# The last 32 columns of a two-layer image kernel kept in SBUF by mask slot, and stored by an indirect DMA in the middle of the output loop

## The chip, the cores and the metric

The kernel runs on one core of a Trainium2 chip. The metric is the device time of one execution in microseconds; the time given for the kernel is the median of several executions. One execution was also taken with the hardware profiler; "the trace" is its record, and all single durations come from it.

## The reference

The input x is one image of 512 x 512 positions with 64 channels, float32. Two layers follow, both residual:

```
# layer 0: x = x + L0(gn(x))
xn    = ln(gn(x))                                  # group norm over the image, layer norm over channels
left  = (xn @ left_w  + left_b)  * mask * sigmoid(xn @ lgate_w + lgate_b)
right = (xn @ right_w + right_b) * mask * sigmoid(xn @ rgate_w + rgate_b)
out   = ln(einsum('bkjd,bkid->bijd', left, right)) @ out_w + out_b
L0    = out * sigmoid(xn @ ogate_w + ogate_b)
# layer 1: x = x + L1(gn(x)); L1 keeps 12 x 12 Fourier modes
x_ft  = fft2(gn(x))[:12, :12];  out_ft = einsum('bcmn,comn->bomn', x_ft, w)
L1    = real(ifft2(out_ft, padded to 512 x 512))
```

`mask[i, j] = m[i] * m[j]` for a sequence mask m of 512 zeros and ones. Group norm has 32 groups of two channels; its statistics run over the whole image, so layer 1 cannot begin its correction before the last tile of layer 0 is done.

## The kernel before, in words

**Slots and ranks.** The kernel sorts the 512 image rows by the mask: a row's *rank* is its place in that order, and a *slot* is a place in it. Layer 0 works on slots, four blocks of 128 (b = 0 to 3) on the 128 partitions. `src_i[:, b, jc]` holds, for each slot, the index of its row's chunk jc of 32 columns in x (row index times 16, plus jc). A tile is one block of 128 rows times 32 columns times 64 channels; in SBUF it has 8 KB on each partition, 1,048,576 bytes in all. There are 16 column chunks (NJ) x 4 blocks = 64 tiles.

**Layer 0's last stage** (the loop over s, lines 1137 to 1251; its order is written out by hand, step by step, and each engine's queue holds the instructions in that order) runs over 32 units, a unit being one column chunk and two blocks: `units[k] = (jc, half)`. A unit is loaded by two gathers (POOL's queue, line 1038) into one of five places of the big SBUF tensor `places` (`x_of(k)`, line 976, ring of RING = 5), is transposed, gated and added up there (POOL's `added`, line 1056; the last unit's end on VectorE, `finished`, line 1060), and stays until three things have read it: TensorE's `transform` (line 1079, the forward row transform with the basis `hb`, which is in slot order), VectorE's `statistics` (line 1109), and the `store` (line 1071), which writes its two tiles to DRAM on SP's queue. The DRAM copy is `x1_h`, two tensors of 256 columns each (line 54), with rows in slot order. Units 0 to 29 are stored at their own step, unit 31 at line 1230 after everything else.

**Layer 1's end** (lines 1253 to 1393). `group_norm_affine` (line 1297) ends the statistics; `mixed_ps` (line 1311) multiplies the modes; `back_columns(jb)` (line 1329) makes the inverse transform along the columns for four chunks (jb = 0 to 3, into `parts`): jb = 0 before the loop, the others inside it. Then the output loop goes over the 64 tiles in the order of the rows of the image: chunk jc outer, block b inner, where b now counts *image rows*, not slots. So each tile has to be fetched from `x1_h` by rank: `fetch_rows` (line 939) is an indirect gather on POOL's queue with `dst_i` (line 832), rank times 8 plus the chunk's place in its tensor. For each tile TensorE multiplies the row basis `rinv` (in row order) with `parts` into four PSUM tiles `l_ps` (line 1377), VectorE adds each to the tile (line 1384), and SP stores the tile directly (line 1385).

```
ahead = 4 * jc + b + AHEAD
if ahead < len(tiles_left):
    fetch_rows(ahead)
```

**What sets the order around the change.** The fetched tiles live in a ring of AHEAD = 15 buffers (`buffers`, lines 933, 1261 to 1265): parts of `places` that are free by then, five tiles `lx_t`, and two spare pieces. Three gathers are issued during the last units (line 1187), twelve after the loop over s (line 1266); in that part the places 0 and 1, which hold units 30 and 31, serve as four buffers once they are stored. In the output loop the gather for position i + 15 is issued after tile i, into tile i's buffer, so POOL waits for that store to land. POOL's queue is in order, and so is SP's. The DMAs of POOL's queue (q0, made by software) use eight semaphores in turn, and so do SP's (q1).

Of the kernel before, what the change touches and what calls it, by code (L numbers as in the profile page):

```python
# [10 lines left out]
I32 = mybir.dt.int32  # L11
# [18 lines left out]
JC = 32  # L30
NJ = N // JC
K = 2 * P
AHEAD = 15
# [13 lines left out]
def conv_preact_kernel(ctx: ExitStack, tc: tile.TileContext, t: dict):  # L47
# [5 lines left out]
    x1_d = dram.tile([N, N, C], F32, name="x1_d")  # L53
    x1_h = [dram.tile([N, HALF, C], F32, name=f"x1_h{h}") for h in range(2)]
    fwd_d = dram.tile([M2, N, C], F32, name="fwd_d")
# [14 lines left out]
    src_i = const.tile([P, 4, NJ], I32, name="src_i")  # L70
    few_i = const.tile([P, NJ // 2], F32, name="few_i")
    n_i = const.tile([1, 1], I32, name="n_i")
    with tc.tile_pool(name="ix", bufs=1) as xp, tc.tile_pool(
# [17 lines left out]
        pick = load_const("c_pick", [P, G])  # L91
        nc.sync.dma_start(few_i, t["c_iota"][:, : NJ // 2])
        nc.vector.tensor_copy(table[:, :, 1], mask_i32)
# [527 lines left out]
    def compact(fc):  # L621
# [201 lines left out]
        with tc.tile_pool(name="tri", bufs=1) as trp:  # L823
# [3 lines left out]

            dst_i = fc.tile([P, 4, NJ // 2], I32, name="dst_i")
            base = fc.tile([P, 4], F32, name="dst_base")
            nc.vector.tensor_scalar(base, rank_p, float(NJ // 2), None, ALU.mult)  # L830
            for b in range(4):
# [49 lines left out]
            with tc.manual_schedule(), tc.tile_pool(name="late", bufs=1) as lp:  # L881
# [50 lines left out]
                free = 3 * 64 * C + C * MODES * MODES  # L932
                buffers = [place(7)[:, JC:], places[:, free : free + JC * C].rearrange("p (n c) -> p n c", c=C)]
                buffers += [place(2)[:, r * JC : (r + 1) * JC] for r in range(2)]
                ranked = [h.rearrange("s (k j) c -> (s k) (j c)", k=NJ // 2) for h in x1_h]
                tiles_left = [(jc, b) for jc in range(NJ) for b in range(4)]
                fetched = {}

                def fetch_rows(i):
                    jc, b = tiles_left[i]  # L940
                    fetched[jc, b] = buffers[i % AHEAD]
                    gather(fetched[jc, b].rearrange("p j c -> p (j c)"), ranked[jc // 8], dst_i, b, jc % 8)

# [3 lines left out]
                with tc.tile_pool(name="np_x", bufs=LEAD + 2) as tp, tc.tile_pool(  # L947
# [123 lines left out]
                    def store(k, r):  # L1071
                        jc, half = units[k]
                        b = 2 * half + r
                        nc.sync.dma_start(
                            x1_h[jc // 8][b * P : (b + 1) * P, (jc % 8) * JC : (jc % 8 + 1) * JC, :].rearrange("p j c -> p (j c)"),
                            x_of(k)[:, r * JC : (r + 1) * JC].rearrange("p j c -> p (j c)"),
                        )
# [59 lines left out]
                    for s in range(-LEAD, total_g + 2 * SIZE):  # L1137
# [3 lines left out]
                        def held(i):  # L1141
                            return 0 <= v - i < len(units)
# [44 lines left out]
                        if (v, n) in ((last - 2, 3), (last - 1, 3), (last, 3)):  # L1187
                            fetch_rows(len(fetched))
                        if v == last and 2 <= n < 6:
# [63 lines left out]
                with tc.tile_pool(name="lq", bufs=1) as qp, tc.tile_pool(name="lx0", bufs=1) as xp0, tc.tile_pool(  # L1253
# [6 lines left out]
                    for i, xp in enumerate(xps):  # L1260
                        buffers += [xp.tile([P, JC, C], F32, name=f"lx_t{i}_{j}") for j in range((2, 2, 1)[i])]
                        if i > 0:
                            buffers += [place(i - 1)[:, r * JC : (r + 1) * JC] for r in range(2)]
                    spare = places[:, 7 * 64 * C - 8 * 2 * MODES * M2 : 7 * 64 * C]
                    buffers += [spare[:, i * JC * C : (i + 1) * JC * C].rearrange("p (n c) -> p n c", c=C) for i in range(2)]
                    for i in range(len(fetched), AHEAD):
                        if i == 8:
                            nc.gpsimd.memset(picks, 0.0)
                        fetch_rows(i)
                    pick4 = qp.tile([P, 4], F32, name="pick4")  # L1270
                    nc.scalar.dma_start(pick4, t["c_pick4"])
# [4 lines left out]
                    with tc.tile_pool(name="sps", bufs=1, space=PSUM) as sps:  # L1276
# [12 lines left out]
                        def join_modes(ab):  # L1289
                            nc.vector.tensor_add(v[:, 0], sums[:, :, :MODES], turned[:, :, MODES:])  # L1290
                            nc.vector.tensor_sub(v[:, 1], turned[:, :, :MODES], sums[:, :, MODES:])
                            for k in range(2):
                                h = slice(k * C, (k + 1) * C)
                                one = v[h, k, 0, 0:1]
                                nc.vector.scalar_tensor_tensor(one, ab[h, 2:3], float(N * N), one, ALU.mult, ALU.add)

                        ab2 = group_norm_affine(lp, sets, 8, "x1c", turn_sums, join_modes)
# [68 lines left out]
                    with tc.tile_pool(name="lpq", bufs=2, space=PSUM) as pq, tc.tile_pool(  # L1366
                        name="lpt", bufs=2, space=PSUM
                    ) as pt, tc.tile_pool(name="lps", bufs=4, space=PSUM) as pp:
                        for jc in range(NJ):
                            for b in range(4):  # L1370
                                it = parts[:, jc // 8, (jc % 8) * N : (jc % 8 + 1) * N]
                                xt = fetched.pop((jc, b))
                                group = []
                                for g in range(4):
                                    ps = pp.tile([P, JC, 16], F32, name="l_ps")
                                    h = slice(32 * g, 32 * g + M2)
                                    nc.tensor.matmul(  # L1377
                                        ps.rearrange("p j o -> p (j o)"), rinv[h, b, :], it[h],
                                        start=True, stop=True, tile_position=(32 * g, 0),
                                    )  # L1380
                                    group.append(ps)
                                for g, ps in enumerate(group):
                                    os_ = slice(16 * g, 16 * g + 16)
                                    nc.vector.tensor_add(xt[:, :, os_], xt[:, :, os_], ps)  # L1384
                                nc.sync.dma_start(  # L1385
                                    out[0, b * P : (b + 1) * P, jc * JC : (jc + 1) * JC, :].rearrange("i j c -> i (j c)"),
                                    xt.rearrange("p j c -> p (j c)"),
                                )
# [82 lines left out]
```

## Time and profile before

| what | value |
|---|---|
| median of 3 runs | 1818.94 us (1818.11 to 1819.47) |
| the profiled execution | 1816.82 us |
| its span, first to last instruction | 1815.0 us |
| TensorE busy | 1641.3 us (90%) |
| VectorE busy | 1424.5 us (78%) |
| ScalarE busy | 961.3 us (53%) |
| POOL busy | 945.1 us (52%) |
| DMA, whole run | 467.94 MB, mean 258 GB/s |
| last VectorE statistics of layer 0 end | 1498.6 us |
| first store of the output loop issued (SP) | 1528.22 us |
| last VectorE add of the output loop ends | 1787.25 us |

The busy shares are means over stages that differ. The page's slices cut the span in 40 pieces of 45.4 us; their digits are busy tenths. The chain of waits follows the work that ended last backwards, from each instruction to what released it. In a timeline line the columns are start, duration (both us), engine, line, operation, output and inputs, count, and in brackets the idle time before it and what ended it. The table by stage gives, for a stretch of time, its length, the busy time and number of instructions of TensorE's matmuls, its weight loads, VectorE, ScalarE and POOL, then TensorE's granted clock, the share of the 16 DMA engines in use, and GB/s.

### The profile page before, as it was taken

Reading aid. Unit: us, or ns where it says so; the run is one execution under the profiler, and the core shown is the slowest. Engines: PE = TensorE matmul, PEld = TensorE weight load, DVE = VectorE, ACT = ScalarE, POOL = GpSimd, SP = SyncE. Lnnn points to the kernel's source line nnn. Section 1 sums busy time; section 2 is a strip of 40 time slices with the busy share of each in tenths; the row PEclk is TensorE's granted clock in tenths of the full one; section 3 lists DMA queues with packets and bytes.
Section 4 is the critical chain, followed back from the end, with each engine's and each line's share of the span. In section 5 each row is a group of like instructions: output and inputs, shape, how many; then the busy total and the mean of one; then the engine's idle time right before and its main releaser. Section 6 shows DMA issues by size and latency. Waiting matters only on the chain. (4 is left out here: it accounts for less than half of the span.)

```text
span 1815.0 us, 33640 instructions
## 1 busy us (share of the span) xinstructions
PE 1641.3 (90%) x11424; PEld 1287.8 (71%) x11424; DVE 1424.5 (78%) x2980; ACT 961.3 (53%) x1708; POOL 945.1 (52%) x711
## 2 busy tenths in 40 slices
PE   6779899999899999998999999999999977998772
PEld 6667666664688778897888888888888844665331
DVE  7989777777455547779999999999999996765442
ACT  3666555554222259986777777777777741011000
POOL 4665111111000006788999999999999892211120
PEclk9989999999899999999999999999999986555555
DMA  7999155556655513577777776777677689999999
GB/s 286 386 386 380 72 138 137 140 140 153 203 176 184 175 47 133 213 256 254 259 239 242 265 246 234 256 267 260 238 259 271 220 261 418 425 427 426 427 426 385
DMA packets 189525, 467.94 MB, mean 258 GB/s; under 512 B 34848, under 2 KB 134176, under 8 KB 148384
## 3 DMA queue, kind: packets, MB, share of 16 engines
q1 hardware_dynamic: 158160, 262.09, 42.5%
q0 software_dynamic: 27712, 201.40, 29.0%
q10 hardware_dynamic: 3472, 2.20, 0.5%
q8 instruction: 93, 1.52, 0.3%
q14 instruction: 88, 0.72, 0.1%
HBM read 278.05 MB, written 187.56 MB: 257 GB/s over the span
## 5 line engine op out<-in xcount | busy, mean ns | idle before, releaser
L995 PE MATMUL w_ps<-gate_x,xt_c 128*128 128x128 f32 x2048 | 281.1, 281 | 28.9 <-DVE z_t L1211 27.3
L1058 POOL TENSOR_TENSOR places<-places,z_t 128x1024 f32<-128x1024 f32 x127 | 301.0, 2370 | 8.1
L995 PEld LDWEIGHTS w_ps<-gate_x,xt_c 128*128 128x128 f32 x2048 | 252.6, 194 | 45.1 <-DVE z_t L1211 43.6
L995 PE MATMUL c_ps<-center_x,xt_c 128*128 128x128 f32 x2048 | 277.6, 279 | 1.2 <-ACT xt_c L1024 0.6
L995 PEld LDWEIGHTS c_ps<-center_x,xt_c 128*128 128x128 f32 x2048 | 253.6, 195 | 3.9 <-ACT xt_c L990 2.8
L1377 PE MATMUL l_ps<-places,rinv 24*128 24x512 f32 x512 | 207.4, 1127 | 30.1 <-DVE places L1384 18.8
L1113 DVE BATCH_NORM_STATS2 stats2c<-places 128x6 f32<-128x128 f32 x1024 | 220.4, 278 | 8.4 <-POOL places L1058 8.4
L1028 DVE TENSOR_REDUCE scratch<-sq_c 128x16 f32<-128x1024 f32 x160 | 194.5, 1216 | 27.9 <-ACT sq_c L1023 19.4
L1215 POOL TENSOR_TENSOR z_t<-z_t,bias_row_out 128x1024 f32<-128x1024 f32 x32 | 75.6, 2364 | 247.8 <-DVE z_t L1211 243.7
L1162 ACT ACTIVATE z_t<-z_t 128x1024 f32<-128x1024 f32 x128 | 135.5, 1058 | 130.6 <-DVE z_t L1217 129.1
L985 PE MATMUL t_ps<-c_ident,places 128*128 128x128 f32 x1280 | 199.6, 279 | 1.3 <-DVE places L870 1.3
L1377 PEld LDWEIGHTS l_ps<-places,rinv 24*128 24x128 f32 x512 | 120.3, 304 | 112.3 <-DVE places L1384 57.0
L985 PEld LDWEIGHTS t_ps<-c_ident,places 128*128 128x128 f32 x1280 | 145.1, 142 | 60.6 <-issue 52.9
L990 ACT ACTIVATE xt_c<-t_ps,ab_xc 128x512 f32<-128x512 f32 x256 | 176.0, 687 | 13.2 <-PE t_ps L985 12.1
L1211 DVE TENSOR_TENSOR z_t<-w_ps,rs_n 128x512 f32<-128x512 f32 x256 | 171.9, 672 | 8.3 <-PE w_ps L995 8.2
L1020 ACT ACTIVATE sq_c<-c_ps 128x512 f32<-128x512 f32 x256 | 150.5, 588 | 32.5 <-PE c_ps L995 32.0
L1217 DVE TENSOR_TENSOR z_t<-z_t,scratch 128x1024 f32<-128x1024 f32 x128 | 156.3, 1221 | 9.9 <-ACT rs_n L1034 3.7
L687 DVE BATCH_NORM_STATS2 stats1c<-x_ps 128x6 f32<-128x512 f32 x256 | 156.6, 682 | 8.0 <-PE x_ps L686 7.6
L1054 POOL TENSOR_TENSOR z_t<-z_t,places 128x1024 f32<-128x1024 f32 x64 | 151.5, 2368 | 13.9 <-ACT z_t L1162 13.8
L1384 DVE TENSOR_TENSOR places<-places,l_ps 128x512 f32<-128x512 f32 x176 | 109.2, 682 | 55.8 <-DMA places<-x_h,dst_i 43.9
L1054 POOL TENSOR_TENSOR z_t<-z_t,bias_row_out 128x1024 f32<-128x1024 f32 x63 | 149.3, 2370 | 5.7 <-ACT z_t L1162 5.4
L749 POOL COPY rbc<-rq_out 128x512 f32<-128x512 f32 x64 | 38.3, 613 | 210.2 <-DVE rq_out L214 132.0
(213 smaller groups left out, 2746.9 us busy)
## 6 DMA issues: line engine op xcount, KB each, us to landing
x_h<-places SPq DMA_DIRECT2D x64, 1024.0 KB
out_x<-places SPq DMA_DIRECT2D x44, 1024.0 KB
places<-u_d SPq DMA_DIRECT2D x512, 64.0 KB
out_x<-lx_t SPq DMA_DIRECT2D x20, 1024.0 KB
left_d<-o_c SPq DMA_DIRECT2D x64, 256.0 KB
right_d<-o_c SPq DMA_DIRECT2D x64, 256.0 KB
left_raw<-left_d SPq DMA_DIRECT2D x64, 256.0 KB
right_raw<-right_d SPq DMA_DIRECT2D x64, 256.0 KB
```

The costliest lines, as they stand in the source:

```text
L687: nc.vector.bn_stats(stats[:, 0, 16 * (jc % quarter) + 4 * r + c, :], ps.rearrange("p i k -> p (i k)"))
L985: nc.tensor.transpose(tps[:, i, :], flat[:, o : o + P], ident)
L990: nc.scalar.activation(xts[s], tps, AF.Identity, bias=ab1[:, 2:3])
L995: nc.tensor.matmul(ps[:, 2 * i : 2 * i + 2, :], xts[s][:, i, :], w, start=True, stop=True)
L1020: nc.scalar.activation(sq, cps, AF.Square)
L1028: nc.vector.tensor_reduce(totals[k % 2][:, 8 * (n - 1) : 8 * (n + 1)], sqs.pop(s // 2), AX.X, ALU.add)
L1054: nc.gpsimd.tensor_mul(zs[k, c], zs[k, c], u)
L1058: nc.gpsimd.tensor_add(xr, xr, zs.pop((k, c)))
L1113: nc.vector.bn_stats(st[k // 4][:, g, k % 4, :], x_of(k)[:, :, 2 * g : 2 * g + 2])
L1211: nc.vector.tensor_mul(z[:, 8 * odd : 8 * odd + 8, :], wps, rs)
L1217: nc.vector.tensor_add(z, z, bias_ps["ogate"].unsqueeze(1).to_broadcast([P, 16, C]))
L1377: nc.tensor.matmul(ps.rearrange("p j o -> p (j o)"), rinv[h, b, :], it[h], start=True, stop=True, tile_position=(32 * g, 0),)
```

## The change

The four tiles of the last chunk (jc = 15; units 30 and 31) are no longer written to `x1_h` and fetched again. They stay in places 0 and 1, in slot order. `x1_h` becomes three tensors of 160 columns (PART = 5 chunks each), and `dst_i` counts with 5 instead of 8. The four kept tiles are the first four buffers of the ring of 15, and stand at positions 11 to 14 of the output loop; eleven tiles are fetched ahead of the loop, into the other buffers, where before there were fifteen. Because the kept tiles are in slot order, they need a row basis in slot order: `rank_inv` is made from `hb` by two scalings and a copy on ScalarE (`by_slot`), four transposes on TensorE, and a copy from PSUM. And their stores must bring each slot to its image row: POOL issues an indirect store with `src_i`. The inner `back_columns` come after positions 4, 13 and 28, for chunks 12 to 15, 4 to 7 and 8 to 11.

```diff
-    x1_h = [dram.tile([N, HALF, C], F32, name=f"x1_h{h}") for h in range(2)]
+    x1_h = [dram.tile([N, PART * JC, C], F32, name=f"x1_h{h}") for h in range((NJ - 1) // PART)]
...
-                buffers = [place(7)[:, JC:], places[:, free : free + JC * C].rearrange("p (n c) -> p n c", c=C)]
+                buffers = [place(i)[:, r * JC : (r + 1) * JC] for i in order[:2] for r in range(2)]
+                buffers += [place(7)[:, JC:], places[:, free : free + JC * C].rearrange("p (n c) -> p n c", c=C)]
                 buffers += [place(2)[:, r * JC : (r + 1) * JC] for r in range(2)]
-                tiles_left = [(jc, b) for jc in range(NJ) for b in range(4)]
-                fetched = {}
+                tiles_left = [(jc, b) for jc in range(NJ - 1) for b in range(4)]
+                tiles_left[AHEAD - 4 : AHEAD - 4] = [(NJ - 1, b) for b in range(4)]
+                fetched = {(NJ - 1, b): buffers[b] for b in range(4)}
 
                 def fetch_rows(i):
                     jc, b = tiles_left[i]
-                    fetched[jc, b] = buffers[i % AHEAD]
-                    gather(fetched[jc, b].rearrange("p j c -> p (j c)"), ranked[jc // 8], dst_i, b, jc % 8)
+                    fetched[jc, b] = buffers[(i + 4) % AHEAD]
+                    gather(fetched[jc, b].rearrange("p j c -> p (j c)"), ranked[jc // PART], dst_i, b, jc % PART)
...
-                        if n == 7 and held(0) and v < last:
+                        if n == 7 and held(0) and v < last - 1:
                             store(v, 0)
-                        if n == 3 and held(1) and v - 1 < last:
+                        if n == 3 and held(1) and v - 1 < last - 1:
                             store(v - 1, 1)
-                        if n == 6 and v - 1 == last:
-                            for r in range(2):
-                                store(last, r)
...
-                        if i > 0:
-                            buffers += [place(i - 1)[:, r * JC : (r + 1) * JC] for r in range(2)]
...
-                    for i in range(len(fetched), AHEAD):
+                    for i in range(len(fetched) - 4, AHEAD - 4):
                         if i == 8:
                             nc.gpsimd.memset(picks, 0.0)
                         fetch_rows(i)
+                    for k, factor in enumerate((1.0, -1.0)):
+                        nc.scalar.mul(
+                            by_slot[:, :, :, k:M2:2],
+                            hb[:, :, k:M2:2].unsqueeze(2).to_broadcast([P, 4, 4, MODES]), factor / (N * N),
+                        )
+                    nc.scalar.copy(by_slot[:, :, :, M2:], hb[:, :, M2:].unsqueeze(2).to_broadcast([P, 4, 4, 32 - M2]))
...
+                            for b in range(4):
+                                nc.tensor.transpose(turned_b[:, b, :], by_slot[:, b].rearrange("p g m -> p (g m)"), ident)
+                            nc.scalar.copy(rank_inv, turned_b)
...
-                        for jc in range(NJ):
-                            for b in range(4):
+                        for i, (jc, b) in enumerate(tiles_left):
+                                kept = jc == NJ - 1
...
-                                        ps.rearrange("p j o -> p (j o)"), rinv[h, b, :], it[h],
+                                        ps.rearrange("p j o -> p (j o)"), (rank_inv if kept else rinv)[h, b, :], it[h],
...
-                                nc.sync.dma_start(
-                                    out[0, b * P : (b + 1) * P, jc * JC : (jc + 1) * JC, :].rearrange("i j c -> i (j c)"),
-                                    xt.rearrange("p j c -> p (j c)"),
-                                )
-                                ahead = 4 * jc + b + AHEAD
+                                if kept:
+                                    nc.gpsimd.indirect_dma_start(
+                                        out=out.rearrange("o h (k j) c -> (o h k) (j c)", k=NJ),
+                                        out_offset=bass.IndirectOffsetOnAxis(ap=src_i[:, b, jc : jc + 1], axis=0),
+                                        in_=xt.rearrange("p j c -> p (j c)"), in_offset=None,
+                                    )
+                                else:
+                                    nc.sync.dma_start(
+                                        out[0, b * P : (b + 1) * P, jc * JC : (jc + 1) * JC, :].rearrange("i j c -> i (j c)"),
+                                        xt.rearrange("p j c -> p (j c)"),
+                                    )
+                                ahead = i + AHEAD
                                 if ahead < len(tiles_left):
                                     fetch_rows(ahead)
-                                if jc % 4 == 1 and b == 0 and jc // 4 < 3:
-                                    back_columns(jc // 4 + 1, pq, pt, False)
+                                if i in (4, 13, 28):
+                                    back_columns((3, 1, 2)[i // 12], pq, pt, False)
```

More of the change, by code (lines that the diff above doesn't have):

```diff
@@ L31 @@
 NJ = N // JC
+PART = 5
 K = 2 * P
@@ L70, in conv_preact_kernel @@
     src_i = const.tile([P, 4, NJ], I32, name="src_i")
-    few_i = const.tile([P, NJ // 2], F32, name="few_i")
+    few_i = const.tile([P, PART], F32, name="few_i")
     n_i = const.tile([1, 1], I32, name="n_i")
@@ L91, in conv_preact_kernel @@
         pick = load_const("c_pick", [P, G])
-        nc.sync.dma_start(few_i, t["c_iota"][:, : NJ // 2])
+        nc.sync.dma_start(few_i, t["c_iota"][:, :PART])
         nc.vector.tensor_copy(table[:, :, 1], mask_i32)
@@ L826, in compact @@
             tri = places.rearrange("p (j r c) -> p j r c", r=2, c=C)
-            dst_i = fc.tile([P, 4, NJ // 2], I32, name="dst_i")
+            dst_i = fc.tile([P, 4, PART], I32, name="dst_i")
             base = fc.tile([P, 4], F32, name="dst_base")
-            nc.vector.tensor_scalar(base, rank_p, float(NJ // 2), None, ALU.mult)
+            nc.vector.tensor_scalar(base, rank_p, float(PART), None, ALU.mult)
             for b in range(4):
@@ L932, in compact @@
                 free = 3 * 64 * C + C * MODES * MODES
-                buffers = [place(7)[:, JC:], places[:, free : free + JC * C].rearrange("p (n c) -> p n c", c=C)]
+                buffers = [place(i)[:, r * JC : (r + 1) * JC] for i in order[:2] for r in range(2)]
+                buffers += [place(7)[:, JC:], places[:, free : free + JC * C].rearrange("p (n c) -> p n c", c=C)]
                 buffers += [place(2)[:, r * JC : (r + 1) * JC] for r in range(2)]
-                ranked = [h.rearrange("s (k j) c -> (s k) (j c)", k=NJ // 2) for h in x1_h]
-                tiles_left = [(jc, b) for jc in range(NJ) for b in range(4)]
-                fetched = {}
+                ranked = [h.rearrange("s (k j) c -> (s k) (j c)", k=PART) for h in x1_h]
+                tiles_left = [(jc, b) for jc in range(NJ - 1) for b in range(4)]
+                tiles_left[AHEAD - 4 : AHEAD - 4] = [(NJ - 1, b) for b in range(4)]
+                fetched = {(NJ - 1, b): buffers[b] for b in range(4)}
                 def fetch_rows(i):
                     jc, b = tiles_left[i]
-                    fetched[jc, b] = buffers[i % AHEAD]
-                    gather(fetched[jc, b].rearrange("p j c -> p (j c)"), ranked[jc // 8], dst_i, b, jc % 8)
+                    fetched[jc, b] = buffers[(i + 4) % AHEAD]
+                    gather(fetched[jc, b].rearrange("p j c -> p (j c)"), ranked[jc // PART], dst_i, b, jc % PART)
                 ends = []
@@ L1074, in store @@
                         nc.sync.dma_start(
-                            x1_h[jc // 8][b * P : (b + 1) * P, (jc % 8) * JC : (jc % 8 + 1) * JC, :].rearrange("p j c -> p (j c)"),
+                            x1_h[jc // PART][b * P : (b + 1) * P, (jc % PART) * JC : (jc % PART + 1) * JC, :].rearrange("p j c -> p (j c)"),
                             x_of(k)[:, r * JC : (r + 1) * JC].rearrange("p j c -> p (j c)"),
@@ L1187, in compact @@
                         if (v, n) in ((last - 2, 3), (last - 1, 3), (last, 3)):
-                            fetch_rows(len(fetched))
+                            fetch_rows(len(fetched) - 4)
                         if v == last and 2 <= n < 6:
@@ L1269, in compact @@
                         fetch_rows(i)
+                    by_slot = places[:, 7 * 64 * C : 7 * 64 * C + 4 * P].rearrange("p (b g m) -> p b g m", b=4, g=4)
+                    rank_inv = places[:, 7 * 64 * C + 4 * P : 7 * 64 * C + 8 * P].rearrange("p (b k) -> p b k", b=4)
+                    for k, factor in enumerate((1.0, -1.0)):
[4 more added lines that the diff above has]
+                    nc.scalar.copy(by_slot[:, :, :, M2:], hb[:, :, M2:].unsqueeze(2).to_broadcast([P, 4, 4, 32 - M2]))
                     pick4 = qp.tile([P, 4], F32, name="pick4")
@@ L1295, in join_modes @@
                                 nc.vector.scalar_tensor_tensor(one, ab[h, 2:3], float(N * N), one, ALU.mult, ALU.add)
+                            turned_b = ps_t.tile([P, 4, P], F32, name="t_ps")
+                            for b in range(4):
+                                nc.tensor.transpose(turned_b[:, b, :], by_slot[:, b].rearrange("p g m -> p (g m)"), ident)
+                            nc.scalar.copy(rank_inv, turned_b)
                         ab2 = group_norm_affine(lp, sets, 8, "x1c", turn_sums, join_modes)
```

## The prediction

> **What bounds the kernel now.** I read the 40 slices first, since the change sits at the end of the program.
>
> ```profile
> DMA  7999155556655513577777776777677689999999
> GB/s 286 386 386 380 72 138 137 140 140 153 203 176 184 175 47 133 213 256 254 259 239 242 265 246 234 256 267 260 238 259 271 220 261 418 425 427 426 427 426 385
> ```
>
> From slice 33 (1497 us) on, the DMA engines are full at 418 to 427 GB/s. Before it they are not. The busy table by stage gives this stage its rate:
>
> ```profile
> 1490.00:1516.00 26.00, 16.66 (x118) 7.81 (x118) 17.74 (x75) 1.24 (x3) 14.81 (x16) 0.68 1.02 402
> 1516.00:1529.00 13.00, 8.42 (x47) 5.65 (x48) 7.76 (x13) 3.50 (x6) 0.00 (x0) 0.67 1.01 420
> ...
> 1560.00:1785.00 225.00, 193.03 (x503) 115.46 (x498) 134.21 (x218) 13.35 (x24) 41.20 (x44) 0.51 1.01 426
> ```
>
> The last columns are DMA share and GB/s: 1.0 and 426 through the whole final loop, while VectorE works 134 of 225 us. A tile of 128x32x64 floats is 1.0486 MB, so **one transfer costs 1.0486 MB / 426 GB/s = 2.46 us**, and a tile (gather plus store) 4.92. But from 1490 to 1529 the loop has not begun; what lets it begin is in the chain of waits:
>
> ```profile
> 1508.95 6.45 PE mixed_ps L1311 x72
> ...
> 1517.48 0.94 PE q_ps L1338 x16
> ...
> 1519.66 2.85 PE it_ps L1356 x16
> ...
> 1523.61 2.12 PE l_ps L1377 x8
> 1525.73 0.68 DVE places L1384
> ```
>
> No DMA stands in it: the statistics, the mode product and the inverse transform end at 1525.7 whatever is moved meanwhile. So the end is bound by two things in turn: an engine chain until the first store, then the DMA engines until 1811 (the span is 1815.0, the profiled execution 1816.82).
>
> **Part 1, bytes removed.** Four x_h stores and four x_h gathers go: 8 x 2.46 = 19.7 us of DMA work. How much of it lies after the loop's start? SP's and POOL's timelines:
>
> ```profile
> 1528.22 8.88 SPq L1385 DMA_DIRECT2D out_x<-places  x4
> ```
> ```profile
> 1510.03 0.93 POOL L637 DMA_INDIRECT places<-x_h,dst_i  x1 [2.19 <-DMA lx_t<-x_h,dst_i]
> 1513.34 0.93 POOL L637 DMA_INDIRECT places<-x_h,dst_i  x1 [2.38 <-DMA lx_t<-x_h,dst_i]
> ...
> 1537.56 0.94 POOL L637 DMA_INDIRECT places<-x_h,dst_i  x1 [22.72 <-DMA out_x<-places]
> ```
>
> The first output store is issued at 1528.22; by the trace's semaphore events it lands at 1536.8, and the two gathers issued at 1510.03 and 1513.34 land at 1531.8 and 1536.5. So when the loop's stores begin, two prefetched tiles are still outstanding, and before has 64 stores + 49 gathers + 2 = 115 transfers to go. The ring keeps 15 tiles: after also starts with 15 on the chip, 11 fetched and 4 kept, and must then move 64 stores + 49 gathers = 113. **Only two of the eight transfers are saved where they count: -4.9 us.** The other six would have run while the engine chain was the bound; the DMA will simply be idle: between 1490 and 1536.5 before moves 26 x 402 + 13 x 420 + two tiles, about 18.0 MB; without eight tiles 9.6 MB is left, done 23 us after 1490, at about 1513. From there to the first store's data it idles some 16 us. Without a backlog the first stores also run with gaps: the gather behind store 0 can be issued only once that store has landed. From a fastest store of 3.8 us from issue to landing (an x_h store, semaphore events) and tiles every 2.85 us, these gaps come to about 1 us. Part 1: **-3.9 us**.
>
> **Part 2, the wait added.** The four kept tiles stand at positions 11 to 14 and are stored by POOL, whose queue is in order and also issues every gather. The list of the changed program's instructions, with what each waits for, shows:
>
> ```
> 825 L1399 DMACopy out_x<-places,src_i 8192x2048 [waits DMASW0_49,DVE_49]
> 826 L638 DMACopy places<-x_h_62,dst_i 128x2048 [waits DMASW1_49,DMASW0_49]
> 827 L1399 DMACopy out_x<-places,src_i 8192x2048 [waits DMASW2_49,DVE_49]
> 828 L638 DMACopy places<-x_h_62,dst_i 128x2048 [waits DMASW3_49,DMASW2_49]
> ```
> ```
> 1511 L1405 DMACopy out_x<-places 128x2048 [waits DMASW5_49,DMASW4_49,DMASW6_49,DMASW2_49,DMAHW6_49,DMASW0_49,DVE_49]
> ```
>
> POOL's DMAs take the semaphores SW0 to SW7 in turn; the kept stores have 0, 2, 4, 6. Each gather (row 826) reuses the buffer just stored and waits for that store to land; the next kept store stands behind that gather. And SP's store of position 15 (row 1511) waits for all four, since an indirect store may write any row of the output. All later SP stores, and through them all gathers from position 30 on, stand behind it. So from the landing of store 10 to that of kept store 14 nothing moves but what POOL issues, **one hop at a time**.
>
> Price of a hop, from rows: a store's landing to the next gather's issue is 0.76 us (1536.80 to 1537.56). The fastest gather of one tile is in the group of line 637:
>
> ```profile
> DMA to landing us min/median/max: 5.4/9.6/23.1
> ```
>
> 5.4 us from the start of its issue, 0.94 of descriptor making included. The kept store is issued 1.24 us after the gather (the spacing of POOL's gathers from 1493.20 on), so its data stands behind the gather's: +2.46. A hop is 0.76 + 5.4 + 2.46 = 8.6 us, in which the DMA works 4.92: **3.7 us idle**. Hops:
> - Into kept store 11: hidden. POOL's rows around the time when store 10 lands are
>
> ```profile
> 1572.19 0.94 POOL L637 DMA_INDIRECT places<-x_h,dst_i  x1 [4.02 <-DVE places L1384]
> 1577.05 0.94 POOL L637 DMA_INDIRECT places<-x_h,dst_i  x1 [3.92 <-DVE places L1384]
> 1582.01 0.94 POOL L637 DMA_INDIRECT lx_t<-x_h,dst_i  x1 [4.02 <-DVE places L1384]
> ```
>
>   (the third is released by store 10). Gathers land 15.0 us after issue there, so two are queued, 5 us of work, over the 3 us until the next has data. With that cover gone: +3.7.
> - Into 12, 13 and 14: 3 x 3.7 = 11.0 us; q0 has run empty and SP is blocked.
> - From 14 to SP's store 15: fastest store 3.8 - 2.46 = 1.4 us.
>
> Part 2: **+12.4 us**. An indirect store is in no row of before. I take a gather's price (same 128 rows of 8 KB, same queue). From below: hops as cheap as SP's, 4 x 1.4 = 5.5. From above: the fastest x_h gather, 6.8 us, gives hops of 5.1 idle, four of them 20.4; and if scattered rows move at the 280 GB/s of the 20 us from 1470, when the weight loads run, 4 x 1.3 = 5.2 more: 25.6.
>
> The Trainium skill ("DMA: Bandwidth & Descriptors", Anatomy of one DMA, SWDGE path) fits a fixed 2.0 us plus bytes/436e3 per DMA; that speaks against the change, since dependent transfers show it openly. As an estimate by that rule a hop idles 2.0 us, four hops 8.0, and the net would be +4.1; the rows here add POOL's wake-up and descriptor making, which the measured 0.76 and 5.4 contain, and I go by them.
>
> **Small parts, at nothing.** ScalarE makes the slot basis with two 128x192 scalings (0.44 us each, row of line 928) and one 128x128 copy (at most as much), after its last statistics work at 1500.9, and is idle until 1518.4. TensorE's four transposes are eight matmuls (sixteen like them, it_ps in the chain above, took 2.85 us: 1.4) and stand after the variance product (ends 1505.2) and before mixed_ps at 1508.95, in 3.75 us of idle time; uncovered they would cost 1.4. ScalarE's copy of the result (1.0) ends long before 1518. The constant loads on ScalarE's queue start 1.3 us later, with less traffic ahead of them. x_h in three parts changes indices and strides (40 KB instead of 64) and no packet size; a store or gather is the same 8 KB a row. Back_columns moves to positions 4, 13 and 28: ahead of its use, and DVE is not the bound there.
>
> **Sum.** -3.9 + 12.4 = **+8.5 us**: 1816.82 becomes 1825.3 by the profiled execution. The median of the runs, 1818.94, lies 2.1 above that execution, so I predict **1827.4 us**.
>
> **Rivals.**
> - *Bytes win (faster).* The hops run in cover, because SP's and POOL's queues hold enough when the chain begins; then -3.9 us alone is left: 1815.0. It decides where the chain's idle time falls under 3.9 us, about 1 us a hop. Against it: q1 holds nothing (row 1511 blocks it) and q0 two gathers. 0.06.
> - *The whole 19.7 us is saved*, 1799: the loop would have to start 16 us earlier, and the chain shows no DMA. 0.02.
> - *Half covered hops*: +1.6 us by the lower bound, 1820.5, no measurable change. 0.10.
> - *Dear hops or slow scatter*: upper bound 25.6 - 3.9 = +21.7, 1840.6; middle 1836. 0.10.
> - That it does not do what it says can be excluded: SP's list has 60 x_h stores, POOL's four out_x stores.
>
> **Numbers.** The forecast case, 1822.6 to 1832, has 0.72. This kernel's measurements can tell 0.2% (3.6 us) from no change. Slower: 0.72 + 0.10 = 0.82; within: 0.10; faster: 0.06 + 0.02 = 0.08. The range 1819 to 1838 takes in the forecast, the half covered hops and most of the dear ones, and leaves out about 0.13.
>
> **What would show it.** DMA idle from about 1513 to 1529; l_ps still starting near 1523.6. Then full share until about 1587, three holes of 3.7 us, 8.6 us apart, with POOL waiting for out_x stores; SP's twelfth out_x store issued near 1613 though its adds ended some 25 us before, a burst of eight behind it, and 426 GB/s from there to the end. No holes, or an earlier l_ps, would make me wrong; so would holes above 5 us.

## The result and the profile after

| what | before | after |
|---|---|---|
| median | 1819.2 us (1818.11 to 1820.61) | 1837.43 us (1833.58 to 1838.85) |
| profiled execution | 1816.82 us | 1836.13 us |
| its span | 1815.0 us | 1834.3 us |
| last DMA packet ends | 1813.6 us | 1832.9 us |

The ratio is 1.0095 (95% interval 1.0082 to 1.0108): the change costs 18.2 us by the medians and 19.3 us by the profiled executions. I had forecast +8.5.

The slices of the page of after, 45.8 us each:

```profile
DMA  7999155556665503676877877677777697889999
GB/s 289 385 371 381 64 138 138 138 138 159 205 182 176 183 24 156 225 243 239 268 250 239 300 250 247 231 265 240 250 268 245 218 283 290 332 342 427 427 427 388
```

Slices 33, 34 and 35 (1513 to 1651 us) were full before; now they carry 290, 332 and 342 GB/s. Everything behind them is full as before. The table by stage shows which parts of these slices are empty (columns as before: TensorE's matmuls, its weight loads, VectorE, ScalarE and POOL, then clock, DMA share and GB/s):

```profile
1490.00:1516.00 26.00, 18.15 (x127) 8.04 (x131) 18.50 (x76) 2.52 (x7) 12.49 (x13) 0.66 0.89 339
1516.00:1529.00 13.00, 7.57 (x53) 5.03 (x46) 7.90 (x13) 3.49 (x6) 0.00 (x0) 0.83 0.17 70
...
1529.00:1580.00 51.00, 46.72 (x157) 32.74 (x154) 32.62 (x52) 9.99 (x21) 9.38 (x10) 0.50 0.97 394
...
1590.00:1600.00 10.00, 10.00 (x32) 7.09 (x30) 8.90 (x15) 0.00 (x0) 1.96 (x2) 0.50 0.60 201
1600.00:1610.00 10.00, 10.00 (x31) 6.80 (x29) 9.21 (x15) 0.00 (x0) 1.94 (x2) 0.50 0.66 228
1610.00:1621.00 11.00, 11.00 (x34) 7.69 (x32) 9.95 (x16) 0.00 (x0) 1.94 (x2) 0.50 0.57 199
...
1645.00:1790.00 145.00, 113.21 (x236) 58.68 (x238) 73.22 (x119) 0.00 (x0) 28.12 (x30) 0.50 1.01 427
```

Two empty stretches: 70 GB/s just ahead of the loop, and about 210 GB/s from 1590 to 1621, while TensorE is busy with other tiles and SP may store nothing. The first is the idle time that I had forecast, but it begins later than I said:

```profile
1510.00:1520.00 10.00, 7.08 (x88) 3.89 (x88) 2.42 (x5) 0.32 (x2) 0.00 (x0) 0.78 0.83 345
1520.00:1530.00 10.00, 7.21 (x32) 5.20 (x34) 6.50 (x12) 3.17 (x6) 0.00 (x0) 0.73 0.04 14
```

By the packet records the DMA runs at its full rate until 1518, where the forecast had it done at 1513. The chain of waits has the same members as before, 0.8 to 1.7 us later, with no DMA among them. (The loop's first add starts anywhere from 1519.4 to 1528.7 us in the profiles of this study.)

```profile
1510.27 6.17 PE mixed_ps L1324 x72
...
1518.67 1.02 PE q_ps L1351 x16
...
1520.93 3.33 PE it_ps L1369 x16
...
1525.35 1.18 PE l_ps L1390 x8
1526.53 0.68 DVE places L1397
```

The second one is the chain of kept stores (line 1399) and gathers (line 638) on POOL's queue; the brackets give POOL's idle time and what ended it:

```profile
1582.50 0.99 POOL L1399 DMA_INDIRECT out_x<-places,src_i  x1 [0.30 <-issue]
1592.71 0.96 POOL L638 DMA_INDIRECT places<-x_h,dst_i  x1 [9.22 <-DMA out_x<-places,src_i]
1593.98 0.99 POOL L1399 DMA_INDIRECT out_x<-places,src_i  x1 [0.30 <-DVE places L1397]
1602.12 0.96 POOL L638 DMA_INDIRECT places<-x_h,dst_i  x1 [7.14 <-DMA out_x<-places,src_i]
...
1611.60 0.96 POOL L638 DMA_INDIRECT places<-x_h,dst_i  x1 [7.23 <-DMA out_x<-places,src_i]
1612.86 0.98 POOL L1399 DMA_INDIRECT out_x<-places,src_i  x1 [0.30 <-DVE places L1397]
1621.36 0.96 POOL L638 DMA_INDIRECT places<-x_h,dst_i  x1 [7.52 <-DMA out_x<-places,src_i]
```

Each gather waits for the kept store in front of it. From gather to gather (1592.71, 1602.12, 1611.60, 1621.36) a hop is 9.41, 9.48 and 9.76 us. SP's twelfth output store comes at the end of the chain, though VectorE had ended its tile at 1589.12:

```profile
1621.23 3.09 SPq L1405 DMA_DIRECT2D out_x<-places  x4
```

To count what this costs I added up the bytes of all packets. "Idle" from here on is the length of a stretch less the time that its bytes take at 426 GB/s.

| stretch | before | after |
|---|---|---|
| 1490 to 1529 us | 1.7 us idle | 16.1 |
| 1529 to 1580 | 0.4 | 4.0 |
| 1580 to 1592.45, kept store 11 lands | | 2.8 |
| three hops to 1601.86, 1611.34 and 1621.10 | | 4.5, 4.5, 4.8 |
| 1621.10 to 1645 | | 2.5 |
| 1580 to 1645 in all | -0.1 | 19.1 |
| bytes after 1529 | 120.0 MB | 118.7 MB |

From 1529 on: +3.6 and +19.2 of idle time, less 1.3 MB or 3.1 us of bytes. That gives +19.7 against the measured +19.3. Of the 16.1 us ahead of the loop 10.6 lie between 1518 and 1529 and 3.8 between 1492 and 1497, before the gathers that POOL issues from 1493.37 on bring data.

### The profile page after: what moved, and what is told of

Same layout as the page of the kernel before. It is cut to its first block, busy times and chain, and to the rows that moved or that the text cites. A ratio compares the mean times of both kernels' runs of the same rounds, so it can differ in the third digit from the quotient of the medians.

```text
span 1834.3 us, 33632 instructions
## 1 busy us (share of the span) xinstructions
PE 1651.8 (90%) x11428; PEld 1286.8 (70%) x11428; DVE 1424.7 (78%) x2980; ACT 963.3 (53%) x1712; POOL 946.1 (52%) x711
## 5 line engine op out<-in xcount | busy, mean ns | idle before, releaser
L1390 PEld LDWEIGHTS l_ps<-places,rinv 24*128 24x128 f32 x480 | 113.4, 302 | 125.9 <-DVE places L1397 75.0
L688 DVE BATCH_NORM_STATS2 stats1c<-x_ps 128x6 f32<-128x512 f32 x256 | 155.6, 680 | 13.1 <-PE x_ps L687 12.3
L1058 POOL TENSOR_TENSOR z_t<-z_t,places 128x1024 f32<-128x1024 f32 x64 | 151.7, 2371 | 13.9 <-ACT z_t L1166 13.8
```

The lines of the kernel that those rows point to most:

```text
L688: nc.vector.bn_stats(stats[:, 0, 16 * (jc % quarter) + 4 * r + c, :], ps.rearrange("p i k -> p (i k)"))
L1058: nc.gpsimd.tensor_mul(zs[k, c], zs[k, c], u)
L1390: nc.tensor.matmul(ps.rearrange("p j o -> p (j o)"), (rank_inv if kept else rinv)[h, b, :], it[h], start=True, stop=True, tile_position=(3 ...
```

## The experiments

My theory after the result: the loss is the chain of dependent indirect stores, during which SP's stores are shut out and the DMA engines find nothing to do; the saved bytes bring little because most of them would have moved while the engine chain set the time anyway. The rivals: an indirect store is slow in itself, or the lost prefetch (eleven gathers and an idle DMA ahead of the loop) costs the time. Kernels measured together share the runs of the kernel before, whose median lay between 1815 and 1819 us on different chips; so I compare by ratios to it. The code below is against the changed kernel unless something else is said.

### The kept stores one behind the other

```diff
-                                if ahead < len(tiles_left):
-                                    fetch_rows(ahead)
+                                if ahead < len(tiles_left) and not AHEAD - 4 <= i < AHEAD - 1:
+                                    for later in range(3, -1, -1) if i == AHEAD - 1 else (0,):
+                                        fetch_rows(ahead - later)
```

> The four kept stores are issued by POOL one behind the other, and the four gathers into their buffers after the last of them; the order is all that changes. They still wait for one another, because each may write any row of the output, and SP's store of position 15 still waits for all four. Theory (the hops cost the time: each exposes a DMA's fixed time while nothing else may move): a hop is now one store alone, about 0.3 us to wake, 1 us of descriptor making and 4.5 us until it has landed, 5.8 us with 2.46 of data, 3.3 idle instead of 4.6; three hops save some 4 us: 1832 to 1835. Rival 1 (the scattered rows themselves are slow to write): the same four scatters, no change, 1837. Rival 2 (the loss is the DMA idle ahead of the loop, with eleven instead of fifteen gathers to run): no change, 1837.

Measured: 1830.85 us, ratio 1.0079 (1.0052 to 1.0106); I had expected 1832 to 1835. The idle time from 1580 to 1645 falls from 19.1 to 13.1 us, but the interval of the ratio overlaps that of the changed kernel. Three stores of POOL's timeline:

```profile
1594.61 0.97 POOL L1399 DMA_INDIRECT out_x<-places,src_i  x1 [9.77 <-DVE places L1397]
1599.92 0.96 POOL L1399 DMA_INDIRECT out_x<-places,src_i  x1 [4.34 <-DVE lx_t L1397]
1605.24 0.96 POOL L1399 DMA_INDIRECT out_x<-places,src_i  x1 [4.35 <-DVE lx_t L1397]
```

They start 5.3 us apart although nothing but stores is in the queue. The profile names VectorE as releaser, but its adds were long done; the semaphore events show each store landing 4.56 us after its start and the next one issued 0.75 to 0.8 later. So an indirect store waits for the indirect store before it. It is not slow: 4.56 us for 1 MB, POOL's own 0.97 us at the issue (the making of the descriptors) included, and the packet records show its data at about 420 GB/s. The first rival falls.

The Trainium skill ("DMA: Bandwidth & Descriptors", Anatomy of one DMA, SWDGE path) fits 2.0 us plus bytes/436e3 to one DMA of this kind; an estimate by it is 4.4 us. The 4.56 us agree with it. The hop of 5.3 us does not follow from it, since POOL's way from the landing to the next issue comes on top.

### One scratch tensor in place of the output

```diff
+        kept_d = dram.tile([NJ * N, JC * C], F32, name="kept_d")
...
-                                        out=out.rearrange("o h (k j) c -> (o h k) (j c)", k=NJ),
+                                        out=kept_d,
```

> The four kept tiles are scattered with the same indices, but into a scratch tensor in DRAM and not into the output, so the last 32 columns of the output are left out; then no store of SP has to wait for them. POOL's order is unchanged, so each gather still waits for a kept store to land. Theory: what cost the time is that SP's stores stood behind the chain. Now SP stores tiles 15 to 25 beside it, 11 x 2.46 = 27 us of work over hops whose idle parts sum to 14, so nearly all of the idle time is filled: about 1819 to 1823. Rival 1 (slow scatter): the scatters are the same; 1835 or more. Rival 2 (idle ahead of the loop, eleven gathers): 1837.

Measured: 1823.1 us, ratio 1.0026 (1.0008 to 1.0043). The last 32 columns of the output are left out. The four indirect stores still wait for one another, but SP does not wait for them.

### Four scratch tensors, one behind the other

Both edits together, with a scratch tensor for each kept tile, so that no indirect store waits for another.

> Both: four scratch tensors, one for each kept tile (the last 32 columns of the output are left out), and the four scatters issued one behind the other with the gathers after them. Now neither SP nor the scatters wait for a scatter. Theory: no hops are left, and the byte count alone stands: 113 transfers after the first store instead of some 114.5, less the gaps at the start of 4 us: 1818 to 1821, at most 2 us under the run with one scratch tensor. Rival 1: 1830 or more. Rival 2: 1837.

Measured: 1821.08 us, ratio 1.0017 (1.0002 to 1.0032).

### No indirect store

```diff
-                                if kept:
+                                if False:
```

> The kept tiles are stored by SP directly, with no scatter: the last 32 columns of the output stay in slot order, so the return to image order is left out. No indirect store is in the kernel; POOL only gathers. Theory: as with four scratch tensors, 1818 to 1821. Rival 1 (slow scatter): the same, so this run alone cannot tell the two apart; against the scratch runs it does. Rival 2 (idle ahead of the loop): that idle time is unchanged, so 1837.

Measured: 1818.43 us, ratio 1.0004 (0.9990 to 1.0018). The stretch of the chain in these three kernels, in the order in which they were told (one scratch tensor, four of them, no indirect store); each line is from that kernel's own table by stage:

```profile
1580.00:1645.00 65.00, 56.02 (x176) 38.23 (x176) 37.24 (x60) 11.34 (x19) 10.59 (x11) 0.53 0.98 402
```
```profile
1580.00:1645.00 65.00, 61.05 (x199) 41.40 (x200) 47.08 (x73) 10.90 (x18) 16.19 (x18) 0.55 1.01 424
```
```profile
1580.00:1645.00 65.00, 61.47 (x194) 41.32 (x193) 47.61 (x76) 8.63 (x15) 12.18 (x13) 0.53 1.01 427
```

402, 424 and 427 GB/s: 3.7, 0.4 and 0 us idle in place of 19.1. Freeing SP alone gives back 15.4 of the 19.1 us of idle time; by the ratios, 1.0095 and 1.0026 from two sets of runs, some 12.5 us of the time. The kernel without an indirect store still prefetches only eleven tiles and still has the idle DMA ahead of the loop (16.7 us from 1490 to 1529), and is as fast as the kernel before. So the lost prefetch is not the loss (the second rival falls), and the eight removed transfers, 19.7 us of DMA work, bring nothing that these runs could tell from zero.

### A 16th buffer, without the indirect store and in the kernel before

Against the kernel without an indirect store:

```diff
-AHEAD = 15
+AHEAD = 16
...
+                    buffers += [place(7)[:, :JC]]
```

`by_slot` and `rank_inv` move to other free places. The same kernel with 15 buffers ran beside it, and the kernel before with the same two lines.

> The kept tiles are stored directly by SP (the last 32 columns of the output stay in slot order, as in the kernel without a scatter), and the ring has a 16th buffer, so that one more tile is gathered ahead of the loop. My theory says that the DMA engines stand idle for 11 to 12 us before the loop's start when no x_h tile is outstanding, so that a transfer moved there costs nothing and saves 2.46 us of the full part: 2 to 3 us under the kernel without a scatter and 15 buffers beside it, so 1815.5 to 1816.5, and the idle time between 1500 and 1529 us falls by about 2.5 us. Rival: what counts is the number of transfers in all, not where they lie; then 16 buffers change nothing, 1818 to 1819.

> The kernel without a scatter once more, unchanged (15 buffers; the last 32 columns of the output stay in slot order), as the pair of the one with 16 buffers on the same chip. Both theories: 1818 to 1819, within 0.1% of the kernel before.

> The kernel before with a 16th buffer. My theory: its DMA engines are full from 1497 us on and two gathers are still outstanding when the loop's stores begin, so one more gather ahead of the loop only lengthens that backlog: no gain, 1818 to 1820. Rival: a deeper ring is worth something by itself (fewer waits of a gather for the store of its buffer); then 2 to 3 us under the kernel before, 1816 to 1817, and the gain of the 16-buffer kernel without a scatter says nothing on the idle time ahead of the loop.

Measured: 1812.18 us, ratio 0.9987 (0.9977 to 0.9996) with 16 buffers; 1813.96 us, 0.9992 (0.9983 to 1.0001) with 15; 1814.49 us, 0.9999 (0.9990 to 1.0008) for the kernel before with 16; the kernel before had 1815.71 us. Ahead of the loop the tables of the kernel with 16 buffers and of the one with 15 show:

```profile
1500.00:1529.00 29.00, 18.43 (x137) 12.07 (x137) 16.89 (x43) 4.06 (x7) 3.86 (x6) 0.74 0.68 280
```
```profile
1500.00:1529.00 29.00, 19.59 (x139) 13.16 (x140) 17.24 (x45) 4.09 (x7) 2.98 (x5) 0.72 0.61 252
```

28 GB/s over 29 us are 0.8 MB more in the idle stretch, most of a tile. Between the two kernels lie 1.8 us by the medians and 0.9 us by the ratios, under the 2 to 3 that I expected, and the intervals overlap. The sign fits the theory (a transfer is worth something only if it leaves the full part). But the kernel before, whose DMA is full there, lies with the same buffer 1.2 us under its own 15-buffer form by the medians and 0.2 by the ratios. A gain of the size that I expected is not shown, and these runs do not decide between theory and rival.

### The kept tiles first

Positions 0 to 3 in place of 11 to 14, the stores one behind the other. `back_columns` for chunks 12 to 15 comes before the loop, that for 0 to 3 after position 3:

```diff
-                tiles_left[AHEAD - 4 : AHEAD - 4] = [(NJ - 1, b) for b in range(4)]
+                tiles_left[:0] = [(NJ - 1, b) for b in range(4)]
...
-                    fetched[jc, b] = buffers[(i + 4) % AHEAD]
+                    fetched[jc, b] = buffers[i % AHEAD]
...
-                                if ahead < len(tiles_left):
-                                    fetch_rows(ahead)
+                                if ahead < len(tiles_left) and i >= 3:
+                                    for later in range(3, -1, -1) if i == 3 else (0,):
+                                        fetch_rows(ahead - later)
```

> The kept tiles stand at positions 0 to 3 of the output loop instead of 11 to 14, with their four indirect stores one behind the other on POOL and the gathers into their buffers after the fourth. My theory: the hops' price is that the DMA engines have nothing else to do while they run, and that SP's first direct store waits for all four. Four hops of 5.3 us as measured in the batched kernel, with 2.46 us of data in each, idle 11 to 12 us, in place of the 19 us of the chain in the middle and of the 4 us of gaps at the loop's start: 1825 to 1828. Rival: the price belongs to the middle of the loop, where queued stores are cut off, and at the start, where nothing is queued, the scatters cost next to nothing: 1819 to 1821.

Measured: 1824.82 us, ratio 1.0047 (1.0032 to 1.0063), 9.1 us over the kernel before beside it. In the table by stage:

```profile
1530.00:1550.00 20.00, 16.36 (x64) 11.35 (x63) 9.27 (x16) 6.68 (x12) 5.30 (x6) 0.59 0.46 190
1550.00:1580.00 30.00, 28.64 (x88) 20.14 (x86) 24.51 (x39) 2.33 (x7) 6.11 (x7) 0.50 0.99 400
```

Here the DMA has no backlog and the stores still cost: 2.9 us idle for each of the first three, 2.1 for the fourth, 12.0 us from 1531 to 1580. The price does not belong to the middle of the loop.

### The kept tiles last

`back_columns` stands after positions 4, 20 and 36 here, for chunks 4 to 7, 8 to 11 and 12 to 15.

```diff
-                tiles_left[AHEAD - 4 : AHEAD - 4] = [(NJ - 1, b) for b in range(4)]
+                tiles_left += [(NJ - 1, b) for b in range(4)]
...
-                    fetched[jc, b] = buffers[(i + 4) % AHEAD]
+                    fetched[jc, b] = buffers[4 + i % (AHEAD - 4)]
...
-                                ahead = i + AHEAD
-                                if ahead < len(tiles_left):
+                                ahead = i + AHEAD - 4
+                                if ahead < len(tiles_left) - 4:
```

> The kept tiles stand at the end of the output loop (positions 60 to 63), their four indirect stores one behind the other, with a ring of 11 buffers for the other 60 tiles; no gather and no store of SP stands behind them. My theory: an indirect store into the output waits until every earlier store has landed, the one before it too, and takes 5.34 us from one issue to the next with 2.46 us of data in it. So it costs 2.9 us each wherever it stands: 4 x 2.9 = 11.5 us over the kernel without a scatter, which equals the kernel before: 10 to 13 us over the kernel before beside it. Rival: what costs is that other work waits behind the scatters; at the end nothing does, and only one drain of SP's stores shows: 1 to 4 us over the kernel before.

> The changed kernel itself once more, as the pair of the kernels beside it: 17 to 19 us over the kernel before on this chip, by all theories.

Measured: 1831.48 us, ratio 1.0099 (1.0068 to 1.0130); the changed kernel beside it 1833.77 us, 1.0105 (1.0079 to 1.0131), 17.4 us over the kernel before by the medians. The kept tiles last cost 15.1 us by the medians and 18 by the ratio, above the 10 to 13 I gave. The table by stage:

```profile
1800.00:1825.00 25.00, 0.00 (x0) 0.00 (x0) 0.00 (x0) 0.00 (x0) 3.88 (x4) 0.50 0.42 173
```

The hops are as expected: issues at 1803.61, 1809.01, 1814.37 and 1819.69, some 5.4 us apart, with 2.9 us idle in each. Two terms were missing. The first indirect store waits for SP's last store to land, and the DMA idles 3.8 us before it is issued. And the span ends 5.8 us after the last packet, where before it was 1.5. The trace shows what fills these 4.4 us: behind POOL's last store stands a DRAIN, an instruction of the program's end (line 1487), and it takes 7.3 us. It ends at 1829.37, 4.8 us after the last store has landed, and the other engines' last instructions come behind it. In the kernel before and in the changed kernel the same DRAIN ends 3.6 us after the landing of POOL's last gather, more than 25 us ahead of the end, under SP's last stores. Why it outlasts the landing is not shown. The ring of 11 buffers is not the price: the DMA stays full from 1580 to 1790. The price stays where nothing waits for the stores, which refutes the rival.

### The order of the rows

I had taken 5.4 us for a gather, and those in the chain took 6.70, 6.76 and 7.06. In this kernel the gathers of the chain read in the order of `src_i`:

```diff
+            near_i = fc.tile([P, 4, PART], I32, name="near_i")
+            near = fc.tile([P, 4], F32, name="near")
+            nc.vector.tensor_scalar(near, slot_t[:, :, 0], float(PART), None, ALU.mult)
+            for b in range(4):
+                nc.vector.tensor_scalar(near_i[:, b, :], few_i, near[:, b : b + 1], None, ALU.add)
...
-                    gather(fetched[jc, b].rearrange("p j c -> p (j c)"), ranked[jc // PART], dst_i, b, jc % PART)
+                    gather(fetched[jc, b].rearrange("p j c -> p (j c)"), ranked[jc // PART], near_i if AHEAD + 11 <= i < AHEAD + 15 else dst_i, b, jc % PART)
```

> In the changed kernel, the four gathers that stand between the kept stores read their rows in the order in which the gathers of layer 0's input read theirs (the index of the slot's source row, as in src_i, in place of the rank): four tiles of the output then hold wrong rows. Theory: these gathers take 6.7 to 7.1 us and not the 5.4 us that I took from an in_x gather because of the order of the rows in DRAM; then they land in about 5.4 to 5.8 us, a hop falls from 9.5 to about 8.3 us, and the kernel is 3 to 5 us faster than the changed kernel beside it. Rival: the gather shares the DMA engines with the indirect store issued 1.24 us behind it, whatever rows it reads; then the hops stay at 9.4 to 9.8 us and the time within 1 us of the changed kernel.

Measured: 1834.57 us, ratio 1.0111 (1.0087 to 1.0135), 0.8 us over the changed kernel beside it. The gathers still take 6.67, 6.85 and 6.44 us, the hops 9.43, 9.60 and 9.14. The order of the rows is not the reason.

### The gather by itself

```diff
+    seen = const.tile([P, 1], F32, name="seen")
...
                                 if kept:
+                                    if b > 0:
+                                        nc.gpsimd.tensor_copy(seen, fetched[tiles_left[i + AHEAD - 1]][:, 0, 0:1])
```

> In the changed kernel POOL reads one element of each partition of the tile fetched between two kept stores before it issues the next kept store, so that in the three hops each gather runs with no other transfer beside it. It measures what one gather from x_h takes by itself. Theory: the gather lands later than the 5.4 us that I took because the indirect store issued 1.24 us behind it shares the DMA engines with its rows; by itself it then lands in 4.4 to 5.4 us, a hop is that plus two wakes of POOL and 4.6 us of store, 10.3 to 11 us, and the kernel is 2 to 5 us slower than the changed kernel. Rival: gathering rows of x_h is slow by itself; then it still lands in 6 to 7 us, hops are 11.8 to 12.8 us, and the kernel is 7 to 10 us slower.

Measured: 1839.16 us, ratio 1.0136 (1.0119 to 1.0153). One hop in POOL's timeline:

```profile
1588.73 0.96 POOL L639 DMA_INDIRECT places<-x_h,dst_i  x1 [9.21 <-DMA out_x<-places,src_i]
1594.45 0.18 POOL L1401 COPY seen<-places 128x1 f32<-128x1 f32 x1 [4.76 <-DMA places<-x_h,dst_i]
1595.20 0.99 POOL L1402 DMA_INDIRECT out_x<-places,src_i  x1 [0.57 <-DVE lx_t L1398]
1600.05 0.98 POOL L639 DMA_INDIRECT places<-x_h,dst_i  x1 [3.86 <-DMA out_x<-places,src_i]
```

By the semaphore events the three gathers land 5.66, 5.75 and 5.97 us after their issue; hops are 11.3 to 11.7 us. That lies between my two theories, and so does the time: 23.9 us over the kernel before beside it, where the changed kernel, which did not run beside it, was 17 to 18 us over its own. A gather alone is 0.3 to 0.6 us slower than the 5.4 us of my row, and with the indirect store behind it in the queue another 1.0 us slower.

## Why the prediction was right in direction and wrong in size

The sum was -3.9 + 12.4; its terms, with what the profile of after measured:

| term | forecast | measured |
|---|---|---|
| bytes saved where they count | -4.9 | -3.1 |
| start gaps | +1.0 | +3.6 |
| hop into kept store 11 | 0, hidden | +2.8 |
| three hops, 12 to 14 | 3 x 3.7 = 11.0 | 4.5 + 4.5 + 4.8 = 13.8 |
| from store 14 to full share | +1.4 | +2.5 |
| sum | +8.5 | +19.6 (times: +19.3) |

**What held.** The DMA idles ahead of the loop, and the loop starts when the engine chain lets it: only the fraction of the removed transfers that lay behind the loop's start could count. (That the idle time comes to the forecast 16 us is luck: it begins at 1518 and not at 1513, and most of the rest of the sum lies before 1497.) The chain bounds the middle, with SP's store of position 15 shut out behind it (forecast near 1613, measured 1621.23; its adds had ended 32 us earlier, forecast 25), and from about 1634 on the DMA is full to the end. The rivals that forecast a gain did not occur: the hops ran uncovered, and the loop did not start earlier. The rival that came is "dear hops" (chance 0.10, middle 1836 us): a hop costs what a gather from x_h costs. Its other half, a slow scatter, did not occur. The small parts stayed at nothing, but for `back_columns` (below): without the indirect store the kernel is as fast as before.

**What failed.** The events came in the forecast order, but nearly every term of the sum was too cheap, and two covers (other transfers that were to hide a wait) did not hold: that of the first hop, and the backlog that was to hide `back_columns`.
- *The hop.* I put it together as 0.76 + 5.4 + 2.46 = 8.6 us. Measured is 0.26 us from a landing to the next issue, 6.70 to 7.06 from there to the landing of the gather, and 2.44 to 2.46 more to that of the kept store. The store's 2.46 held, and the wake was dearer in my row. The term that failed is the gather: 5.4 us was the fastest of all gathers of in_x. The fastest x_h gather, 6.8 us, stood beside it in the text as the upper bound, and is what the chain shows. The packet records of the hop from 1592 to 1603 us, in 40 slices, show why a gather costs more than its bytes:

```profile
DMA  0000000099375989989796799999799310000000
GB/s 0 0 0 0 0 0 0 0 179 209 89 209 179 357 357 417 328 298 357 238 328 209 328 447 447 447 387 447 298 387 447 149 60 30 0 0 0 0 0 0
```

  A slice is 0.28 us. The gather's rows begin at 1594.2, 1.5 us after its issue, and come at 90 to 420 GB/s; 447 is reached only from 1598 on; the rows of the kept store issued at 1593.98 are in the later slices too. Of the 1.3 to 1.7 us above my 5.4, the kernel with the gather by itself puts 0.3 to 0.6 down to the gather and about 1.0 to the store behind it.
- *The first hop.* Two gathers did cover its beginning, as forecast, but not all. I had read 15.0 us from issue to landing off the kernel before; with less of a backlog in the queues these two landed after 10.6 and 8.8 us, and the DMA stays below 110 GB/s from 1590 until the store has landed. The store landed 9.95 us after its issue, and 2.8 us were empty.
- *Start gaps.* There are two, not one. The first is that of the forecast (3.0 us from 1529 to 1541, of which 0.9 lie ahead of the first store's data: that store is issued at 1529.02, 0.8 us later than before). The second (0.8 us from 1553 to 1559) comes from `back_columns` after position 4, which keeps VectorE from adding for 9.4 us. I had put that at nothing because VectorE is not the bound there; the cover was the backlog of the DMA queues, and Part 1 had just taken it away.
- *Bytes.* 118.7 MB were moved after 1529 in place of 120.0: 1.3 of a transfer, where I had counted two outstanding gathers from their landings. A gather in flight at that time is partly done.

The measured 1837.43 us lies just inside the stated range of 1819 to 1838, and the upper bound of 25.6 - 3.9 = +21.7 holds the result, in part by luck: 5.2 us of it stand for a slow scatter, which did not occur, and they make up for the bytes and the start gaps, 4.4 us dearer than forecast. My choice between 5.4 and 6.8 us was made for the faster row, though the other was of the same tensor and the same index.

No kernel here that does the whole work beats the kernel before. Of those with indirect stores into the output the best, with the kept tiles first, is 0.47% slower (0.32 to 0.63). Not tried: an indirect store with a view of the output so narrow that SP's stores need not wait for it.

## What to carry to other kernels

Ask of an indirect store what the program takes it to write: here the whole output, so that every direct store behind it on another queue, every gather behind those, and the next indirect store waited for it. Freeing SP's stores of that wait alone gave back 15 of 19 us of idle time. Price removed transfers by the stage in which they would have run: eight of them were 19.7 us of DMA time and 3 us of the end, and the gaps at the loop's start took the 3 us back. And price a chain of dependent transfers from landings of the same tensor in a queue as empty as the chain will be, with each cover that the change itself takes away counted again.

## What the runs showed of the hardware that I had not expected

- An indirect store alone (128 rows of 8 KB) lands in 4.56 us, an indirect gather alone in 5.66 to 5.97 us. The store's rows move at about 420 GB/s from the start, the gather's rise from about 160 to 430 GB/s over some 2 us.
- Behind the chain SP's stores are ready all at once, and its issues grow from 0.33 us to 1.2 to 1.9 us each; for the first 13 us after the chain 2.4 us of the DMA's time stay empty.
- With indirect stores at the very end the span ended 5.8 us after the last packet, against 1.5 us with direct ones: POOL's closing DRAIN ended 4.8 us after the last indirect store had landed, and 3.6 us after POOL's last gather where direct stores of SP came last and hid it.
